# A Mamba-2, MLP and mixture-of-experts layer on one core: the first MLP four steps later, and other banks for early sums and transposes

## The chip, the cores and the metric

One core of one Trainium2 chip runs the whole program in one launch. The number that counts is device time in microseconds, as the median of several runs; lower is better. The engines named below are PE (TensorE: matrix products and transposes), DVE (VectorE), ACT (ScalarE), POOL (GpSimd) and SP (SyncE, which here only issues DMAs). Each works through its own list of instructions in order, and waits on semaphores for the others. [...]

## The reference, cut to what matters

The input x has 2048 tokens of 512 numbers. All arithmetic is fp32.

```
h   = layernorm(x); h1 = rmsnorm(h, ln1_w)
z, xb, B, C, dt = split(h1 @ in_proj_w)        # 512 -> 1024 + 256 + 256 + 1024 + 16
xb, B, C = silu(causal_conv4(xb, B, C))
dt  = softplus(dt + dt_bias);  dA = dt * -exp(A_log)
# 16 chunks of 128 tokens, 16 heads of 64, state 64 x 64 per head:
Y   = C B^T * exp(cum differences of dA) * dt @ xb  +  C @ state * exp(cum dA)
state = exp(sum dA) * state + B^T (decay * dt * xb)
y   = rmsnorm((Y + D * xb) * silu(z), norm_w) @ out_proj_w      # 1024 -> 512, "po" below
h   = h + y
x   = x + h + mlp(rmsnorm(h, ln2_w))            # silu(. @ gate) * (. @ up) @ down, 2048 wide
out = x + experts(layernorm(x))                 # 8 experts of width 352, the best 2 per token
```

## The kernel before

**Blocks and chunks.** The Mamba part runs over 8 blocks of 256 tokens (`TB`), each of two chunks of 128 (`t` = 0 to 15). For a block, `prepare(b)` computes the norm's scales, transposes the two chunks of normed tokens (`transposed`, tile `pt`, into `hT`), the step sizes dt (`pdt`, L228, and a chain of some twenty small DVE operations, L238 to L259, ending in `dA`), and their running sums (`pc`, L262, `pn`, `psum`). `spread(b, j)` brings these sums back from HBM broadcast to all partitions: two DMAs `cum` and four `ec`, with a POOL select behind each `cum`. `project` makes the channels xb, B, C (tiles `pm`, six pairs, weights `wi` loaded by SP in three buffers, each pair with a convolution of eight DVE operations and a SiLU on ACT); `gate` makes z (tiles `pz`, four pairs, with SiLU).

**A chunk's pieces.** `chunk` is a generator of nine pieces: the score products `psc` (L400), the exponentials (L406, ACT) and their products (L408, DVE); the state's part of Y (`py`, L423), then the chunk's own part (`py`, L431) and the new state `pst`; both for two halves of the heads; then the squares for the norm, `po` (L475, eight products of 512 columns), the norm's scale `ry` from `pms` (L478, a square root on ACT), h (L484, which reads `po`), h's own scale r (again a square root), and as the ninth piece the transposes of h into `h2T`, which feed the MLP.

**The MLP.** `feed_forward(fb)` works on 512 tokens (two blocks), also as a generator: 16 column groups of four pieces and one closing piece, 65 in all. It uses seven products where a plain computation would use eight (sums of blocks, made by `sums` and on POOL for the weights). Two banks, `px` and `py_c` (kinds "g" and "u" in `use`, pool `ps_x`), take these products; `pd` (kind "d", pool `ps_mm`) takes the down projection. Nothing uses "g" and "u" before the first MLP starts.

**The order.** `mamba(b)` has 32 steps. In each, some of a chunk's pieces, some projections of the next block and some of `prepare(b + 1)` are issued, and after it the main loop calls `advance()`, which issues one piece of the MLP that is in turn. The first MLP begins in block 2 (`BPF` = 2), when its 512 tokens are done:

```
        for n, _ in enumerate(mamba(b)):

            if b > BPF or b == BPF and n > 1:
                advance()
```

Until block 2 a scheduler orders PE's instructions by its own costs and priorities; from block 2 on (`manual_schedule`, L887) PE's order is the order in which the program issues them. DVE, ACT and POOL are ordered by the scheduler all the way, and the small table loads of ACT (for exponential, SiLU and square root) come wherever its order changes from one function to another. MLP pieces that are left over when block 7 is done run behind it, before the last MLP and the routed experts.

**Banks.** Pool `ps_tr` has one buffer, tag "tr": the transposes of normed tokens, of h and of xb, `pdt`, `pc`, `pn`, `psum`, `pst` and `pms` follow each other in it. `ps_mm` has two, for `pm`, `pz` and `pd`. `ps_y` has one, for `py` and `po`, and at the very start for 20 transposes of the identity that depend on nothing else (L178). `ps_sg` has the scores (two banks wide), `ps_x` one for each of "g" and "u".

Line numbers in this document are those of the kernel before.

Of the kernel before, what the change touches and what calls it, by code (L numbers as in the profile page):

```python
# [8 lines left out]
F32 = mybir.dt.float32  # L9
# [6 lines left out]
P = 128  # L16
T = 2048
D = 512
NK = D // P
# [4 lines left out]
TB = 256  # L24
NCH = TB // P
NB = T // TB
FB = 512
NFB = T // FB
DFF = 2048
FH = FB // 2  # L30
FC = 128
NFC = DFF // FC
NE = 8
# [11 lines left out]
C_CW, C_CB, C_NW, C_D, C_L1, C_L2, C_DTB, C_AL = 0, 48, 60, 68, 76, 80, 84, 100  # L45
# [4 lines left out]
def mamba_mlp_moe(ctx, tc, x, w_in, w_out, w_gu, w_down, par, wr, wg, wu, wd, out):  # L50
# [3 lines left out]
    nc = tc.nc  # L54

    def bc(ap, axis, n):
        ap = ap.unsqueeze(axis)
        shape = list(ap.shape)
        shape[axis] = n
        return ap.to_broadcast(shape)  # L60
# [15 lines left out]
    def load_x(t):  # L76
        res[t] = xp.tile([P, D], F32, name=f"x{t}", tag="x")
        nc.sync.dma_start(out=res[t], in_=x[t * P : (t + 1) * P, :])

    params = pw.tile([P, NPAR], F32, name="params")  # L80
# [20 lines left out]
    ident = const.tile([P, P], F32, name="ident")  # L101
# [66 lines left out]
    ps_y = psa_stack.enter_context(tc.tile_pool(name="ps_y", bufs=1, space=PSUM))  # L168
# [3 lines left out]
    def bank(kind, shape, name):  # L172
        pool, tag = use[kind]
        return pool.tile([P, *shape], F32, name=name, tag=tag)

    idle = ps_y.tile([P, P], F32, name="idle", tag="y")
    for _ in range(20):
        nc.tensor.transpose(idle, ident, ident)  # L178

# [4 lines left out]
        nc.scalar.activation(rboth[:, lo:hi], mv[:, lo:hi, 1], AF.Sqrt, bias=eps2, scale=1.0 + EPS)  # L186
        nc.vector.reciprocal(rboth[:, lo:hi], rboth[:, lo:hi])

    def transposed(src, dst, weight=None):

        pt = bank("tr", [NK, P], "pt")
        for k in range(NK):
            nc.tensor.transpose(pt[:, k, :], src[:, k * P : (k + 1) * P], ident)  # L193
        if weight is None:
            nc.scalar.copy(dst, pt)  # L195
        else:
            nc.vector.tensor_tensor(dst, pt, bc(weight, 2, P), ALU.mult)
# [3 lines left out]
    def prepare(b):  # L201

        nonlocal first_rows
        hT = wa.tile([P, NK, TB], F32, name=f"hT{b}", tag="hT")
        hns = []
        with tc.issue_after(first_rows) if b == 1 else ExitStack():
            scales(b)
            for j in range(NCH):
                t = b * NCH + j
# [5 lines left out]
            first_rows = normed.ins  # L215
        for j in range(NCH):
            yield
            transposed(hns[j], hT[:, :, j * P : (j + 1) * P], params[:, C_L1 : C_L1 + NK])

        yield hT  # L220
        lo, hi = b * NCH, (b + 1) * NCH
# [38 lines left out]
        n = NCH * NH  # L260
# [30 lines left out]
    def spread(b, j, rows_d):  # L291

        t = b * NCH + j
        heads = rows_d[:, j * NH : (j + 1) * NH, :]
        cum = []
        for gp in range(2):
            c = wa.tile([P, 8, P], F32, name=f"cum{t}_{gp}", tag="cum", bufs=3)
            nc.sync.dma_start(out=c, in_=bc(heads[0, 8 * gp : 8 * gp + 8], 0, P))

            nc.gpsimd.affine_select(  # L300
                out=c, in_=c, pattern=[[0, 8], [1, P]], compare_op=ALU.is_ge, fill=-3.0e38,
                base=0, channel_multiplier=-1,
            )
            cum.append(c)
        ec = None
        if t:
            ec = wa.tile([P, 2, 4, P], F32, name=f"ec{t}", tag="ec")
            for g in range(4):
                part = slice(g % 2 * HD, (g % 2 + 1) * HD)
                nc.sync.dma_start(out=ec[part, g // 2], in_=bc(heads[1, 4 * g : 4 * g + 4], 0, HD))  # L310
        return cum, ec

    def finish(steps):
        while True:
            try:
                next(steps)
            except StopIteration as end:
                return end.value
# [36 lines left out]
    def gate(b, pair, hT, zs):  # L355

        pm = ps_mm.tile([P, 2, TB], F32, name=f"pz{b}_{pair}", tag="mm")
        finish(projected(b, 6 + pair, pm, hT))
        nc.scalar.activation(zs[:, 2 * pair : 2 * pair + 2, :], pm, AF.Silu)

    def channels(b):
        xb = wa.tile([P, 4, TB], F32, name=f"xb{b}", tag="xb")
        return xb, [None, None]
# [4 lines left out]
    def turned_x(t, xb):  # L368

        tok = slice(t % NCH * P, (t % NCH + 1) * P)  # L370
        pt = ps_tr.tile([P, 4, P], F32, name=f"ptx{t}", tag="tr")
        for m in range(4):
            nc.tensor.transpose(pt[:, m, :], xb[:, m, tok], ident)
        xbt = wa.tile([P, 2, 4, HD], F32, name=f"xbt{t}", tag="xbt")
        nc.scalar.copy(xbt.rearrange("p a g d -> p (a g d)"), pt.rearrange("p a q -> p (a q)"))
        return xbt
# [4 lines left out]
    def chunk(b, j, dt, ncum, dtdec, cd, cum, ec, xb, cs, zs):  # L381

        nonlocal summed
        t = b * NCH + j
# [4 lines left out]
        y = zs[:, :, tok]  # L389
# [80 lines left out]
                summed = nc.gpsimd.tensor_tensor(sq[:, 0:n, :], sq[:, 0:n, :], sq[:, n : 2 * n, :], ALU.add).ins  # L470
        yield

        po = ps_y.tile([P, D], F32, name=f"po{t}", tag="y")
        for m in range(8):
            nc.tensor.matmul(po, y[:, m, :], w_o[:, m, :], start=(m == 0), stop=(m == 7))  # L475
        yield
# [18 lines left out]
        if off == 0:  # L495
            h2T[fb] = (wk if fb % 2 else wa).tile([P, 2, NK, FH], F32, name=f"h2T{fb}", tag="h2T", bufs=1)
        half, off = divmod(off, FH)
        transposed(h, h2T[fb][:, half, :, off : off + P], params[:, C_L2 : C_L2 + NK])


# [168 lines left out]
    def sums(fb):  # L669
# [3 lines left out]
        b11, b21, b12, b22 = h[:, 0, :KH], h[:, 0, KH:], h[:, 1, :KH], h[:, 1, KH:]  # L673
        ts = wk.tile([P, 3, KH, FH], F32, name=f"ts{fb}", tag="ts", bufs=1)
        nc.vector.tensor_tensor(ts[:, 0], b12, b11, ALU.subtract)
# [12 lines left out]
    def feed_forward(fb):  # L688
# [20 lines left out]
        for c in range(NFC):  # L709
# [8 lines left out]
            if c > 1 and c % 2 == 0:  # L718
                pair = [made.pop(n) for n in (c - 2, c - 1)]
            a = wk.tile([P, 2, FH], F32, name=f"a{fb}_{c}", tag="a", bufs=4)  # L720
            up = wk.tile([P, FH], F32, name=f"up{fb}_{c}", tag="up", bufs=2)
            x1 = bank("g", [FH], f"px{fb}_{c}")
            x2 = bank("u", [FH], f"py{fb}_{c}")
# [58 lines left out]


    coming = prepare(0)
    for _ in range(3):
        hT = next(coming)
    next(coming)
    xc = channels(0)
    ready = None
    for pair in range(6):  # L790
        finish(project(0, pair, hT, *xc))
        if pair < 2:
            next(coming)
        elif pair == 2:
            ready = finish(coming)
            near = [spread(0, j, ready[-1]) for j in range(NCH)]
            nc.sync.dma_start(out=w_o, in_=w_out.rearrange("(t p) n -> p t n", p=P))
    xbts[0] = turned_x(0, xc[0])

    unweighted = list(range(8))  # L800
# [9 lines left out]
    def mamba(b):  # L810

        nonlocal ready, xc, ninth
        hT, dt, ncum, dtdec, cd, _ = ready
        xb, cs = xc
        zs = wa.tile([P, 8, TB], F32, name=f"zs{b}", tag="zs", bufs=1)
        if b + 2 < NB:
            load_x((b + 2) * NCH)
        more = b + 1 < NB
        if more:
            coming = prepare(b + 1)  # L820
            xc = channels(b + 1)
        n = 0
        for j in range(NCH):
            pieces = chunk(b, j, dt, ncum, dtdec, cd, *near[j], xb, cs, zs)
            for _ in range(4):

                if n < 2:
                    halves = (gate(b, pair, hT, zs) for pair in (2 * n, 2 * n + 1))
                elif more:
                    halves = project(b + 1, n - 2, next_hT, *xc)  # L830
                else:
                    halves = iter(())
                next(pieces)
                if more and n == 0:
                    next(coming)
                if more and n == 3:
                    next(coming)
                if b == 0:
                    weigh(1)
                yield  # L840
                next(pieces)
                if n % 4 == 0:
                    finish(ninth)
                next(halves, None)
                yield
                if more and n < 3:
                    next(coming)
                elif more and n == 3:
                    ready = finish(coming)
                next(halves, None)  # L850
                if b == 0:
                    weigh(2)
                yield
                if more and n == 0:
                    next_hT = next(coming)
                yield
                n += 1
            ninth = pieces
            if j == 0 and b + 2 < NB:
                load_x((b + 2) * NCH + 1)  # L860
            if more:
                near[j] = spread(b + 1, j, ready[-1])

    BPF = FB // TB
    ninth = iter(())
    flow = []
    tail = iter(())
# [13 lines left out]
    for b in range(NB):  # L881
        fb, at = divmod(b, BPF)
        if fb and at == 0:
            flow.append([feed_forward(fb - 1), 4 * NFC + 1])
        if b == BPF:

            in_order.enter_context(tc.manual_schedule(engines={mybir.EngineType.PE}))  # L887
        for n, _ in enumerate(mamba(b)):

            if b > BPF or b == BPF and n > 1:  # L890
                advance()
    for n in range(flow[0][1]):
        if n == 2:
# [284 lines left out]
```

## Time and profile before

| | |
|---|---|
| median of 5 runs | 1581.91 us (1580.07 to 1583.02) |
| the profiled execution | 1580.18 us, span 1578.1 us |
| mean granted clock of PE in it | 0.991 |
| PE busy | 1535.3 us, 97% |
| DVE, ACT, POOL busy | 776.8, 753.2, 403.1 us |
| bytes moved by DMA | 218.68 MB, mean 139 GB/s |
| PE idle in 0 to 60 us | 12.4 us |
| PE idle in 200 to 220 us, and granted clock there | 6.64 us, 0.74 |

The span is the time from the first to the last instruction that the profiler saw; the device time is 2.1 us longer. All times within the profile count from the span's start. Matmul records are counted twice in it (each fp32 product appears as two). A granted clock of 1.00 is full speed, and 0.50 half. "Idle before" an instruction is put down to the event that came last, so the name of a releaser is a hint, not a proof. Blocks 0 and 1 take the first 200 us, the blocks with an MLP beside them run to about 1050, the last MLP to about 1240, and the rest is experts.

### The profile page before, as it was taken

Reading aid. Unit: us, or ns where it says so; the run is one execution under the profiler, and the core shown is the slowest. Engines: PE = TensorE matmul, PEld = TensorE weight load, DVE = VectorE, ACT = ScalarE, POOL = GpSimd, SP = SyncE. Lnnn points to the kernel's source line nnn. Section 1 sums busy time; section 2 is a strip of 40 time slices with the busy share of each in tenths; the row PEclk is TensorE's granted clock in tenths of the full one; section 3 lists DMA queues with packets and bytes.
Section 4 is the critical chain, followed back from the end, with each engine's and each line's share of the span. In section 5 each row is a group of like instructions: output and inputs, shape, how many; then the busy total and the mean of one; then the engine's idle time right before and its main releaser. Section 6 shows DMA issues by size and latency. Waiting matters only on the chain. (4 is left out here: it accounts for less than half of the span.)

```text
span 1578.1 us, 19196 instructions
## 1 busy us (share of the span) xinstructions
PE 1535.3 (97%) x6303; PEld 1051.6 (67%) x6303; DVE 776.8 (49%) x2018; ACT 753.2 (48%) x1346; POOL 403.1 (26%) x510
## 2 busy tenths in 40 slices
PE   7899979999999999999999999999999999999997
PEld 6666666777666777767676777666777666555553
DVE  6876755754556364646555554434453352222221
ACT  3988896735663678457748543222211221111110
POOL 3542324423341212111212112011111123333331
PEclk8999989999999999999999999999999999999999
DMA  8443435544554443434344533238776233333332
GB/s 290 154 140 119 137 116 184 184 158 150 183 182 145 163 170 117 131 118 138 119 166 149 167 99 102 84 103 297 241 242 226 86 61 61 66 62 67 67 67 33
DMA packets 127456, 218.68 MB, mean 139 GB/s; under 512 B 11584, under 2 KB 71488, under 8 KB 127360
## 3 DMA queue, kind: packets, MB, share of 16 engines
q1 hardware_dynamic: 105088, 166.08, 32.5%
q0 software_dynamic: 8736, 20.45, 6.9%
q10 hardware_dynamic: 13536, 30.94, 5.2%
q8 instruction: 52, 0.85, 0.2%
q14 instruction: 44, 0.36, 0.1%
HBM read 176.01 MB, written 41.42 MB: 138 GB/s over the span
## 5 line engine op out<-in xcount | busy, mean ns | idle before, releaser
L685 PE MATMUL pd<-md,a 128*128 128x512 f32 x512 | 238.4, 592 | 0.0
L326 PE MATMUL pm<-hT,wi 128*128 128x256 f32 x768 | 187.2, 389 | 1.5 <-DMA wi<-in_w_in 1.5
L326 PEld LDWEIGHTS pm<-hT,wi 128*128 128x128 f32 x768 | 143.4, 194 | 26.6 <-issue 6.9
L686 DVE TENSOR_TENSOR r<-r,pd 128x512 f32<-128x512 f32 x128 | 87.6, 684 | 139.4 <-PE pd L685 138.7
L685 PEld LDWEIGHTS pd<-md,a 128*128 128x128 f32 x512 | 97.0, 190 | 74.1 <-issue 66.2
L347 DVE SCALAR_TENSOR_TENSOR ca<-pre,params,ca 128x256 f32<-128x256 f32 x288 | 134.2, 525 | 0.2
L701 PE MATMUL py<-h2T,ms 128*128 128x256 f32 x512 | 131.6, 379 | 1.6 <-POOL ms L527 0.8
L326 PE MATMUL pz<-hT,wi 128*128 128x256 f32 x512 | 118.5, 384 | 0.0
L1034 PE MATMUL epg<-ew,xgT 128*128 x312 | 118.1, 460 | 0.4 <-ACT xgT L195 0.2
L1034 PE MATMUL epu<-ew,xgT 128*128 x312 | 117.8, 459 | 0.0
L766 POOL TENSOR_TENSOR a<-a,up 128x256 f32<-128x256 f32 x64 | 46.8, 731 | 277.1 <-DVE up L760 239.0
L475 PE MATMUL po<-w_o,zs 128*128 128x512 f32 x256 | 112.8, 593 | 0.0
L406 ACT ACT_TABLE_LOAD x76 | 97.5, 1283 | 28.7 <-DVE ncum L274 19.2
L1055 PE MATMUL epd<-ew,ehT 128*128 (+1 forms) x234 | 107.1, 593 | 1.0 <-DVE ehT L1048 1.0
L701 PEld LDWEIGHTS py<-h2T,ms 128*128 128x128 f32 x512 | 95.6, 190 | 16.9 <-POOL ms L527 1.2
L326 PEld LDWEIGHTS pz<-hT,wi 128*128 128x128 f32 x512 | 95.9, 192 | 15.4 <-issue 1.9
L406 ACT ACTIVATE cum<-cum,ncum 128x128 f32<-128x128 f32 x256 | 86.3, 393 | 5.6 <-POOL cum L300 3.3
L475 PEld LDWEIGHTS po<-w_o,zs 128*128 128x128 f32 x256 | 48.2, 190 | 56.9 <-issue 55.4
L1015 POOL DMA_INDIRECT xg<-xnd,idx x39 | 38.8, 995 | 176.0 <-PE pt L193 174.0
L1034 PEld LDWEIGHTS epu<-ew,xgT 128*128 128x128 f32 x312 | 59.3, 190 | 33.0
L195 ACT COPY xgT<-pt 128x512 f32<-128x512 f32 x39 | 22.8, 587 | 117.7 <-PE pt L193 117.7
L1061 POOL DMA_INDIRECT out<-ey,idx x39 | 61.9, 1587 | 66.8 <-DVE ey L1060 40.8
(248 smaller groups left out, 2568.3 us busy)
## 6 DMA issues: line engine op xcount, KB each, us to landing
wi<-in_w_in SPq DMA_DIRECT2D x80, 512.0 KB, 3.6
ms<-late SPq DMA_DIRECT2D x48, 512.0 KB, 3.6
mg<-early SPq DMA_DIRECT2D x48, 384.0 KB, 3.6
md<-in_w_down SPq DMA_DIRECT2D x64, 256.0 KB, 3.8
cum<-rowsd SPq DMA_DIRECT2D x32, 512.0 KB, 4.1
late<-ms ACTq DMA_DIRECT2D x16, 512.0 KB, 2.7
ec<-rowsd SPq DMA_DIRECT2D x60, 128.0 KB, 3.8
xnd<-xn ACTq DMA_DIRECT2D x28, 256.0 KB, 3.5
```

The costliest lines, as they stand in the source:

```text
L326: nc.tensor.matmul(pm[:, m, :], w[:, k, m * P : (m + 1) * P], hT[:, k, :], start=(k == 0), stop=(k == NK - 1))
L347: nc.vector.scalar_tensor_tensor(ca, pre[:, m, k : k + TB], cw[:, k : k + 1], ca, ALU.mult, ALU.add)
L406: nc.scalar.activation(lt[:, half, i], lt[:, half, i], AF.Exp, bias=ncum[:, j, h : h + 1])
L475: nc.tensor.matmul(po, y[:, m, :], w_o[:, m, :], start=(m == 0), stop=(m == 7))
L685: nc.tensor.matmul(pd, a[:, j * P : (j + 1) * P], d, start=(m == 0), stop=(m == 1))
L686: nc.vector.tensor_tensor(rows[j], rows[j], pd, ALU.add)
L701: nc.tensor.matmul(ps, w[:, k], m[:, k], start=(first and k == 0), stop=(k == KH - 1), skip_group_check=True)
L766: nc.gpsimd.tensor_tensor(a[:, 1], a[:, 1], up, ALU.mult)
L1015: nc.gpsimd.indirect_dma_start(out=xg, out_offset=None, in_=src, in_offset=bass.IndirectOffsetOnAxis(ap=idx[:, n : n + 1], axis=0))
L1034: nc.tensor.matmul(ps, xT[:, k, :], w[:, lo : lo + EI], start=(k == 0), stop=(k == NK - 1))
L1055: nc.tensor.matmul(pd, hT[:n, m, :], w[:n, NG + m * D : NG + (m + 1) * D], start=(m == 0), stop=(m == len(ET) - 1))
L1061: nc.gpsimd.indirect_dma_start(out=out, out_offset=bass.IndirectOffsetOnAxis(ap=idx[:, n : n + 1], axis=0), in_=y, in_offset=None, compute ...
```

## The change

Four edits, one patch.

1. The second of block 0's two sets of transposes goes to a bank of `ps_mm` (kind "d") instead of the "tr" bank, and five more transposes of the identity, into `ps_y`, follow it.
2. The `spread` of block 0's second chunk is issued behind the six projection pairs of block 0 instead of behind the third.
3. `po` of the first four chunks (blocks 0 and 1) goes to the bank "g" instead of `ps_y`.
4. The first MLP piece is issued behind the seventh step of block 2 (`n > 5`) instead of the third (`n > 1`); the ninth piece of chunk 3, which in other blocks is issued in the second quarter of a block's first step group, is issued in block 2 at the end of it, three steps later. All later MLP pieces move with the first, so nine instead of five are left over behind block 7.

```diff
+BPF = FB // TB
...
-    idle = ps_y.tile([P, P], F32, name="idle", tag="y")
-    for _ in range(20):
-        nc.tensor.transpose(idle, ident, ident)
+    def idling(n):
+        idle = ps_y.tile([P, P], F32, name="idle", tag="y")
+        for _ in range(n):
+            nc.tensor.transpose(idle, ident, ident)
+
+    idling(20)
...
-    def transposed(src, dst, weight=None):
-
-        pt = bank("tr", [NK, P], "pt")
+    def transposed(src, dst, weight=None, kind="tr"):
+
+        pt = bank(kind, [NK, P], "pt")
...
-            transposed(hns[j], hT[:, :, j * P : (j + 1) * P], params[:, C_L1 : C_L1 + NK])
+            kind = "d" if b == 0 and j else "tr"
+            transposed(hns[j], hT[:, :, j * P : (j + 1) * P], params[:, C_L1 : C_L1 + NK], kind)
+            if b == 0 and j:
+                idling(5)
...
-        po = ps_y.tile([P, D], F32, name=f"po{t}", tag="y")
+
+        po = ps_y.tile([P, D], F32, name=f"po{t}", tag="y") if t >= BPF * NCH else bank("g", [D], f"po{t}")
...
-            near = [spread(0, j, ready[-1]) for j in range(NCH)]
+            near = [spread(0, 0, ready[-1])]
             nc.sync.dma_start(out=w_o, in_=w_out.rearrange("(t p) n -> p t n", p=P))
+    near.append(spread(0, 1, ready[-1]))
...
-                if n % 4 == 0:
+                if n % 4 == 0 and (b != BPF or n):
                     finish(ninth)
...
                 yield
+                if b == BPF and n == 0:
+                    finish(ninth)
                 n += 1
...
-            if b > BPF or b == BPF and n > 1:
+            if b > BPF or b == BPF and n > 5:
                 advance()
```

More of the change, by code (lines that the diff above doesn't have):

```diff
@@ L862, in mamba @@
                 near[j] = spread(b + 1, j, ready[-1])
-    BPF = FB // TB
     ninth = iter(())
```

## The prediction

> **What bounds the kernel now.** I read the page first: the busy line, then the slices (one is 39.5 us).
>
> ```profile
> PE 1535.3 (97%) x6303; PEld 1051.6 (67%) x6303; DVE 776.8 (49%) x2018; ACT 753.2 (48%) x1346; POOL 403.1 (26%) x510
> ...
> PE   7899979999999999999999999999999999999997
> ...
> ACT  3988896735663678457748543222211221111110
> ...
> PEclk8999989999999999999999999999999999999999
> ```
>
> PE is the bound: 97% busy, and nearly all of what it misses lies in slices 1 and 2 (the start), 6 (197 to 237 us) and 40 (the end, which the change leaves alone). An edit that only reorders PE work is therefore worth the PE idle time that it removes, plus the half-clock time that follows such idle time. ACT, 48% busy over all, is near 90% in slices 2 to 6, so it can take PE's place there.
>
> Next, who PE waited for (total, times, longest):
>
> ```profile
> PE pt L193 <- DVE mv L145: 7.1, 1, 7.1
> PE py L423 <- POOL halo L340: 3.8, 2, 2.4
> PE pc L262 <- POOL pre L339: 3.4, 1, 3.4
> PE pt L193 <- DVE hT L197: 1.9, 1, 1.9
> PE pt L193 <- ACT xbt L375: 1.7, 1, 1.7
> ```
>
> The five sum to 17.9 us; the timeline places them at 199.6, 121.1 and 197.0, 24.8, 7.3 and 41.2. Third, the timeline around the largest (start, length, what; in brackets the idle time before it):
>
> ```profile
> 197.58 0.75 DVE L484 SCALAR_TENSOR_TENSOR h<-po,ry,h 128x512 f32<-128x512 f32 x1
> ...
> 198.43 1.13 PE L423 MATMUL py<-ec,sdiag 128*128 128x128 f32 x8 [1.39 <-POOL halo L340]
> ...
> 204.04 0.29 ACT L139 ACTIVATE r<-m,singles 128x1 f32<-128x1 f32 x1
> ...
> 206.04 0.46 DVE L492 TENSOR_SCALAR h<-h,r 128x512 f32<-128x512 f32 x1
> ...
> 206.64 1.09 PE L193 MATMUL pt<-ident,h 128*128 128x128 f32 x4 [7.08 <-DVE mv L145]
> ...
> 207.52 5.00 PE L326 MATMUL pz<-hT,wi 128*128 128x256 f32 x16
> ...
> 220.38 1.08 PE L431 MATMUL py<-cum,xbt 128*64 128x512 f32 x4
> ```
>
> The 7.08 us is chunk 3's last step: its h is ready at 206.50 (206.04 + 0.46), and PE's written order has nothing in front of it but work already done. The name DVE mv is only the last event seen. The 1.39 us is a bank: L423 starts 0.10 after the read of po at L484 ends (198.33), for po and py share the one buffer of ps_y. The same pair stands at 123.49 (L484 ends at 123.39), where the wait is 2.43. Fourth, stretches of PE alone (length, busy, matmuls, granted clock, DMA share, GB/s):
>
> ```profile
> 1.50:2.50 1.00, 0.97 (x5) 1.00 0.58 199
> ...
> 8.00:9.10 1.10, 0.00 (x0) 0.92 0.87 175
> ...
> 11.00:12.70 1.70, 1.66 (x8) 0.50 1.07 406
> ...
> 199.00:202.00 3.00, 0.56 (x6) 0.68 0.23 89
> 202.00:206.00 4.00, 0.00 (x0) 0.50 0.38 133
> ```
>
> Idle time costs twice: the clock falls to half in the gap at 7.3 and recovers near 19; it falls in the gap at 199.6 and is full again by 212.
>
> **Part 1: first transposes in two banks, five idle transposes.** Before, the second set of four waits for the hT product at L197 (8.41 to 9.09) to free the one "tr" bank, so it runs at 9.14 and its own product at 10.29, behind two hn products (L211, 1.00 for both) that DVE's order put between. After, the second set follows the first at 7.3 in an "mm" bank, which nothing uses yet. DVE's new order has both products in a row: 8.41, 9.00, done at 9.69. So pdt (L228) starts at 9.75, not 11.04: 1.29 earlier. The five idle transposes (4.33/20 = 0.22 each, 1.1) lie in the 1.9 us between and cost nothing; without that gap they cost 1.1.
>
> What follows depends on the clock. At half, pdt takes its 3.60 again and the 3.44 wait of pc at 28.24 just ends 1.29 sooner. At full, pdt takes 1.85 (as at 64.96). The 8 matmuls of pm_0, done at about 20.4 (its copy starts at 20.52), take 3.62 (as at 71.79) and end near 15.2; the DVE chain from there to dA (21.21 to 28.1, 6.9) ends near 22.9, so pc comes 5.2 earlier. DVE's order also puts the statistics of chunk 4 (2.29 waiting for a DMA at 17.1) behind dA; that wait lay before 21.21, so it is no extra. Behind pc the new order has pm_5 between two halves of ptx and the next hn transposes later. That removes 1.73 (ptx's bank) and, as wi leaves SP's queue ahead of the moved spread, 1.48 (wi). It adds about 1.2 before py, whose eight exponentials ACT spreads between SiLUs: 2.0 net, 1.7 taken. The term lies between 3.0 (half clock) and 6.9 (full). The gap of 0.77 at 5.85 left the clock at 1.00 and the 1.87 gap did not; after, the gap is 0.75, but pdt is thin work. I take 4.5; for the range, 0 (DVE at 17.5 and ACT at 19.3 of 20 us busy in 40 to 60 allow nothing) to 7.
>
> [...]
>
> **Part 2: second chunk's spread later.** Two cum DMAs (512 KB), four ec DMAs (128 KB) on SP, and two selects on POOL (1.09 each) move behind the projections of block 0. SP now issues wi for pairs 5 and 6 ahead of cum1_0 (before: 39.93, behind an ec issue of 37.46); counted in part 1. Chunk 1 first needs cum1_0 at about 71 (its first exponential); issue near 33 and 4.1 to land leave over 30 us of cover. Cost 0; if cover were gone, 4.1 + 1.09.
>
> **Part 3: po of chunks 0 to 3 in bank "g".** No instruction more. L423 no longer waits for L484: 2.43 at 123.49 goes (1.39 at 198.43 is counted below). What could be late next: ec is done at 117.1, sdiag at 108.1, and chunk 2's h transposes need ry, which stood on ACT behind three exponentials and a table load (119.78, 0.98, and 1.28) that the new order puts after it. So I take all 2.4; bounds 0 and 2.43. A new wait, po's for the read of the po before, has 25 us of cover or more (po at 111.25, the read before it at 86.3). The first MLP product in that bank comes about 24 us after the last read.
>
> **Part 4: first MLP four steps later, chunk 3's last step after three more.** PE's new order in block 2, walked with the old durations from the shared point (psc ends at 197.0): py 1.05 to 198.1 without the bank wait; pz_0 3.62 to 201.7; hn transposes 0.60; pz_1 3.62 to 205.9. DVE is busy with cum (to 204.3) and xd (205.4), then r's reciprocal, hT 0.69 (206.3), h 0.46 (206.7). The second hn set runs at 206.4, its hT on DVE behind 0.54 and 0.67 at 208.0 to 208.7; h's transposes end at 209.4; py 1.08, pst 1.03, psc 1.13 to 212.6; the next py waits for yd (1.12 behind 0.69 + 0.69) and ends at 213.8; pz_2 3.62, pdt 1.85, pz_3 3.62: 222.8. Before, pz_3 ends at 235.76 with seven products of the MLP's first piece in front of it, 0.865 apart, 6.1: equal to 229.7. Gain 6.9. It is the two waits (8.5) and the half clock (pz_0 5.00 against 3.62, pt 1.09 against 0.60: 1.9), less 3.5 of new waits on DVE and ACT. The moved pieces come back behind block 7: four more, 9.8 (1048.22 to 1057.99), with as much less in the blocks between; PE is full there, so the net is 0. ACT's queue is what stands behind: from 206.2 to the SiLU of pz_3 it has 8 table loads (1.28) and 5.3 of work, 221.7, one us ahead of PE. Bounds: 0 to 8.8.
>
> SP's and POOL's orders around FB boundaries shift by one piece; the waits there are nine of 0.5 to 0.85, so ±1.5; I take 0.
>
> **Sum.** 4.5 + 2.4 + 6.9 = 13.8. The profiled execution took 1580.18 (span 1578.1, 2.1 around it), 1.7 below the median of 1581.91. So 1566.4 beside that one, 1568.2 in median.
>
> **Rivals.** *Front gives nothing* (DVE and ACT bound 40 to 60): 1581.9 - 9.3 = 1572.6. For: those busy shares. Against: ACT is idle for 9.5 of the 20 us before that (10.54 busy in 20 to 40). *The clock stays full*: front 7 and block 2 near 8: 1564. *Block 2 gains only half*, a new wait at py or pdt taking the rest: 1572. *Slower*: ACT bounds block 2. It is busy 19.56 of 20 us in 200 to 220; if pz_3 still ends at 235.8, the 6.1 taken out of PE there leaves a hole, and comes back after block 7. The start's gains then drain into the same wait on ACT: 1581.9 + 6.1 = 1588. It decides once pz_3 ends 6.9 (the other two terms) later than 229.7. Against: ACT's sum above. *It doesn't act*: po's bank moves the wait only; the cover of part 3 excludes that.
>
> **How the numbers follow.** About 0.2% (3.2 us) is the least that can be told from no change. Forecast 0.50 (1565 to 1571), front nothing 0.15, clock full 0.13, half of block 2 0.12, slower 0.07, other losses that cancel the gain 0.03. Faster 0.90, same 0.03, slower 0.07. The range takes the sums with the ends: 1560 (7 + 2.4 + 8.8 + 1.5 off gives 1562.2, and the runs of one kernel spread by some 2 below their median) to 1577 (5 of 13.8 left).
>
> **What would show it.** Right: in the waits of PE the 7.1 of pt and both py L423 rows are gone; pdt starts before 10; MLP products begin after pz_3, near 215 on the new axis; clock 1.00 from 200 to 220. Wrong: a PE wait of over 3 us on ACT or DVE in 200 to 240, or pc not earlier than 27. I am wrong most easily where DVE's and ACT's written orders turn a short delay into a long one.

## The result, and the profile after

The changed kernel took 1587.16 us in the median of 22 runs (1582.48 to 1591.81), the kernel before 1582.17 us beside it (43 runs, 1579.17 to 1585.17): a ratio of 1.0032, with a 95% interval of 1.0025 to 1.0038. It is 5.0 us slower; the forecast was 13.8 us faster, with a range that ended at 1577.

The profiled execution took 1585.92 us (span 1583.9), 5.7 above that of before. Its page, busy line and three slices (line numbers of the changed kernel are up to 10 higher than those of before):

```profile
PE 1538.8 (97%) x6308; PEld 1049.9 (66%) x6308; DVE 780.7 (49%) x2018; ACT 749.4 (47%) x1343; POOL 403.2 (25%) x510
...
PE   8999989999999999999999999999999999999996
...
ACT  5988987645744775557367542222211221111110
...
PEclk9999999999999999999999999999999999999999
```

At this grain the start and block 2 look better (slices 1, 2 and 6 of PE), only the last slice reads one lower, and PE is as busy as it was. The loss shows only in PE's waits (what was waited for: total, times, longest):

```profile
PE pt L197 <- ACT cd L295: 5.2, 3, 2.4
PE py L709 <- DVE a L742: 3.5, 1, 3.5
PE pc L269 <- DVE dA L266: 3.2, 3, 1.9
PE px L709 <- ACT a L754: 3.1, 5, 1.9
PE pt L197 <- DVE hT L201: 2.6, 2, 2.3
```

The rows that the prediction wanted gone are gone: the 7.1 us of h's transposes, both waits of the state product for the y bank, the 3.4 us of `pc`. But the first two rows here are new, and they stand where the prediction did not look, behind block 2. The timeline of PE from the last score products in front of block 2 (start, length, what; in brackets the idle time before it; an fp32 product of PE makes two records, the eight of `po` in 16 chunks 256 on the page, and numbers of its products below are numbers of records):

```profile
189.74 1.13 PE L407 MATMUL psc<-cs,xb 64*128 64x512 f32 x4
...
202.40 0.80 PE L197 MATMUL pt<-ident,h 128*128 128x128 f32 x4 [2.33 <-DVE hT L201]
...
213.71 3.70 PE L333 MATMUL pz<-hT,wi 128*128 128x256 f32 x16
...
228.38 0.41 PE L269 MATMUL pc<-tri,dA 128*32 128x128 f32 x2 [1.55 <-ACT xbt L382]
...
234.36 1.13 PE L709 MATMUL px<-ts,mg 128*128 128x256 f32 x4 [1.93 <-ACT a L754]
```

The same score products in the kernel before:

```profile
195.91 1.13 PE L400 MATMUL psc<-cs,xb 64*128 64x512 f32 x4
```

Here ends block 1's part: PE has by then done the same work in both kernels, but for the five idle transposes. The changed kernel is 6.2 us ahead (190.87 against 197.04). Its last gate products end at 217.41, against 229.7 in the kernel before for the same work (the prediction's figure): 12.3 us ahead, of the 13.8 forecast. Then two waits of ACT, 3.5 together, come within 20 us. How the lead goes on is read from the start of each chunk's `pms`, changed kernel less before, with 9.8 us added from chunk 5 on, since four MLP pieces fewer lie in front of it (the four last ones, 1048.22 to 1057.99 in the trace of before). Chunk 3's `pms` is 8.4 us earlier, but that is not for equal work: ten more records of projections, 2.2 us, are still to come behind it.

| chunk | block 1's end | 5 | 8 | 10 | 11 | 12 | 13 | 14 | 15 |
|---|---|---|---|---|---|---|---|---|---|
| us, for equal work | -6.2 | -9.0 | -6.7 | -8.1 | -5.4 | -2.5 | -1.6 | +4.0 | +5.7 |

So 6.2 us were won up to block 1's end, block 2 added 2.8 net (6.1 up to the gate products, of which 3.3 went again behind them), and 14.7 were lost between chunks 5 and 15. Behind chunk 15 nothing changes any more. Between 240 and 1080 us PE is idle for 12.2 us after and 4.7 before; the stretches below (length, PE busy, matmuls, granted clock, DMA share, GB/s), PE alone, of the changed kernel, show the rest, a clock below full:

```profile
480.00:560.00 80.00, 77.05 (x338) 1.00 0.46 153
...
700.00:860.00 160.00, 156.47 (x657) 0.99 0.40 134
860.00:1000.00 140.00, 136.46 (x572) 0.98 0.36 115
```

In the kernel before, the same three stretches have 79.34, 160.00 and 139.24 us busy and a clock of 1.00. One hundredth of 160 us and two of 140 are some 4 us, so 7.5 + 4 of the 14.7 are seen directly; the rest is spread thinly, or within what one profiled execution differs from another. The largest single wait, by engine (PE's row after DVE's and POOL's, all of the same 10 us):

```profile
968.56 2.36 DVE L665 TENSOR_TENSOR v<-o,oh 128x256 f32<-128x256 f32 x2
970.84 2.08 DVE L666 TENSOR_TENSOR v<-v,wt 128x256 f32<-128x256 f32 x2
972.85 1.81 DVE L668 TENSOR_TENSOR v<-v,place 128x256 f32<-128x256 f32 x2
974.59 0.67 DVE L694 TENSOR_TENSOR r<-r,pd 128x512 f32<-128x512 f32 x1
975.18 0.41 DVE L742 TENSOR_TENSOR a<-a,py 128x256 f32<-128x256 f32 x1
...
968.43 2.81 POOL L477 TENSOR_TENSOR sq<-sq 128x512 f32<-128x512 f32 x3 [6.41 <-ACT sq L475]
971.19 2.85 POOL L402 TENSOR_TENSOR ec<-ec,cs 128x512 f32<-128x512 f32 x2
...
975.65 2.07 PE L709 MATMUL py<-h2T,ms 128*128 128x256 f32 x4 [3.54 <-DVE a L742]
977.51 1.91 PE L709 MATMUL px<-ts,ms 128*128 128x256 f32 x4
```

PE waits for a small MLP addition on DVE (L742), and that stands in DVE's list behind six products `v` of the routing step. The six take 6.25 us here; elsewhere they take 2.3 (median 0.42 each). Meanwhile POOL is at work on a chunk's squares and on `ec`. Behind the wait the granted clock is 0.50 (974.5 to 981.0): four products (two groups of them) that need 1.03 take 2.07 and 1.91.

The second kind of new wait, three times, around 545 us (ACT's rows, then PE's):

```profile
542.18 1.28 ACT L140 ACT_TABLE_LOAD   x1
543.48 0.29 ACT L140 ACTIVATE r<-m,singles 128x1 f32<-128x1 f32 x1
543.79 1.28 ACT L289 ACT_TABLE_LOAD   x1
545.09 0.20 ACT L289 ACTIVATE dtdec<-psum 128x32 f32<-128x32 f32 x1
545.18 0.35 ACT L295 ACTIVATE cd<-psum 64x16 f32<-64x16 f32 x2
...
539.95 0.30 PE L287 MATMUL psum<-dA,late 128*128 128x32 f32 x2
...
545.59 0.66 PE L197 MATMUL pt<-ident,xn 128*128 128x128 f32 x4 [2.44 <-ACT cd L295]
```

`psum` and the routing step's transposes use the same one bank "tr", which comes free when ACT has read `psum` (545.53). The kernel before has the same ACT rows, 16.5 us later (`psum` at 556.49, `cd` done at 562.08); but its PE had a down projection of four products and `pl` in between and came to those transposes only at 563.10, one us after the bank was free. Nothing became slower. The MLP, with the routing steps that ride on it, came four pieces later against the Mamba steps, and now meets them elsewhere.

### The profile page after: what moved, and what is told of

Same layout as the page of the kernel before. It is cut to its first block, busy times and chain, and to the rows that moved or that the text cites. A ratio compares the mean times of both kernels' runs of the same rounds, so it can differ in the third digit from the quotient of the medians.

```text
span 1583.9 us, 19202 instructions
## 1 busy us (share of the span) xinstructions
PE 1538.8 (97%) x6308; PEld 1049.9 (66%) x6308; DVE 780.7 (49%) x2018; ACT 749.4 (47%) x1343; POOL 403.2 (25%) x510
## 5 line engine op out<-in xcount | busy, mean ns | idle before, releaser
L354 DVE SCALAR_TENSOR_TENSOR ca<-pre,params,ca 128x256 f32<-128x256 f32 x288 | 138.2, 538 | 0.3
L333 PEld LDWEIGHTS pz<-hT,wi 128*128 128x128 f32 x512 | 94.8, 190 | 13.8 <-ACT zs L366 0.8
L754 ACT COPY a<-px 128x256 f32<-128x256 f32 x64 | 23.6, 369 | 142.9 <-PE px L709 124.7
```

The lines of the kernel that those rows point to most:

```text
L333: nc.tensor.matmul(pm[:, m, :], w[:, k, m * P : (m + 1) * P], hT[:, k, :], start=(k == 0), stop=(k == NK - 1))
L354: nc.vector.scalar_tensor_tensor(ca, pre[:, m, k : k + TB], cw[:, k : k + 1], ca, ALU.mult, ALU.add)
```

## The experiments

Three theories. *Lag*: parts 1 to 3 give what they give, and the loss behind block 2 comes from the MLP and the routing steps standing four pieces later against the Mamba steps. *Lists*: the new orders on DVE, ACT and POOL, which the scheduler makes from the whole program, cost the time, whatever the lag. *One queue*: a single resource, the bank "tr" or DVE beside POOL, makes the loss. The kernel before took 1582.6 us beside the first four runs, 1582.92 beside the next four, 1582.37 beside the last four.

**Parts 1 to 3 alone.** The changed kernel without part 4: the MLP begins where it did before.

```diff
-            if b > BPF or b == BPF and n > 5:
+            if b > BPF or b == BPF and n > 1:
...
-                if n % 4 == 0 and (b != BPF or n):
+                if n % 4 == 0:
...
-                if b == BPF and n == 0:
-                    finish(ninth)
```

> Parts 1 to 3 (two banks and five idle transposes, the later spread, po in bank g); the first MLP starts where it did before. Theory 'lag': the early gains are real and the loss comes from the MLP running one column group later. Then chunk 3's norm product pms is again about 8.4 us earlier than before, the 7 us wait for chunk 3's h stays, no wait above 1 us stands behind 540 us, and the time is 1582.2 - 8.4 = 1573.8 (1571 to 1577). Rival 'lists': the new orders of DVE, ACT and POOL that come with parts 1 to 3 make the late waits; then waits above 2 us stand behind 540 us and the time is 1582 to 1587.

Measured: 1573.65 us (1571.78 to 1575.26), ratio 0.994 (0.9927 to 0.9952). Its lead is 2.7 us at block 1's end in this execution (chunk 3's `pms` is 5.4 us earlier, not 8.4), and from chunk 5 to chunk 15 its `pms` are 5.4 to 4.6 us ahead, flat. Behind 540 us no wait reaches 0.8 us up to 1080. The wait for h stays, shorter:

```profile
200.23 1.08 PE L197 MATMUL pt<-ident,h 128*128 128x128 f32 x4 [4.81 <-DVE h L500]
```

So block 2 gave 2.7 us here without part 4, and 2.8 in the changed kernel with it.

**Part 4 alone.** The reverse of it: the kernel before with the MLP and chunk 3's last step later.

```diff
-            if b > BPF or b == BPF and n > 1:
+            if b > BPF or b == BPF and n > 5:
...
-                if n % 4 == 0:
+                if n % 4 == 0 and (b != BPF or n):
...
+                if b == BPF and n == 0:
+                    finish(ninth)
```

> The kernel before with part 4 alone: first MLP behind the seventh step of block 2, chunk 3's last step later. Lag: the early gains of parts 1 to 3 (8.4) are missing and the late loss is there: 1587.2 + 8.4 = 1595.6 (1588 to 1598), with waits above 2 us behind 540 us. Lists: the wait for h goes and nothing is given back: 1582.2 - 4 to 7 = 1575 to 1578.

Measured: 1594.24 us (1589.74 to 1596.86), ratio 1.0066 (1.0052 to 1.0081). Part 4 costs 11.6 us by itself and 13.5 on top of parts 1 to 3. Its new waits are those of the changed kernel (what, total, times, longest):

```profile
PE pt L194 <- ACT cd L289: 4.4, 2, 2.5
...
PE py L702 <- DVE a L735: 3.5, 1, 3.5
```

**The lag made up within block 2.** Four steps of block 2 issue two MLP pieces, so from block 3 on everything stands as before.

```diff
             if b > BPF or b == BPF and n > 5:
                 advance()
+            if b == BPF and n in (13, 18, 23, 28):
+                advance()
```

> The changed kernel, with four of block 2's later steps (13, 18, 23, 28) issuing two MLP pieces instead of one, so that from block 3 on MLP and Mamba stand to each other as before. Lag: the gain of 12.3 us that stood at pz_3 of block 2 is kept, less the two waits of 226 to 234 us (3.5): 1570 to 1574, and the waits of 2.4 (545.6), 2.3 (850.7) and 3.5 us (975.6) are gone. Lists: about 1587, with those waits.

Measured: 1578.05 us (1575.32 to 1580.9), ratio 0.9967 (0.9954 to 0.9979). From chunk 5 on its `pms` are flat, 0.5 to 0.9 us behind those of before; the waits of 2.4 and 3.5 us are gone. So the loss behind block 2 is the lag's. But block 2 keeps nothing either: in this execution PE was level with before (0.2 us behind) at block 1's end and is 0.5 behind at chunk 5. The time is 4.4 us above that of parts 1 to 3 alone.

**The lag made up in block 3.**

```diff
             if b > BPF or b == BPF and n > 5:
                 advance()
+            if b == BPF + 1 and n in (5, 13, 21, 29):
+                advance()
```

> The changed kernel, whose MLP makes up its four pieces in the next block (block 3, one extra piece at each of four steps eight apart) and not within block 2; from block 4 on the MLP and the routing steps stand against the Mamba steps as before. Theory (the loss behind block 2 comes from the lag alone; what the front and block 2 gave is kept once the lag is gone): in the changed kernel chunk 5's states' products came 18.8 us earlier than before with about 9.8 us less MLP in front of them, so 9.0 us are there to keep, and no late waits: 1573 (1570 to 1577), and the waits of over 2 us at 545, 850 and 975 us gone. Rival (the pieces made up cost their time again wherever they are put, as they seemed to in block 2): 1577 to 1583. Rival (the loss sits in the new order of the lists, whatever the lag): 1585 to 1588.

Measured: 1577.91 us (1574.06 to 1578.22), ratio 0.9961 (0.9949 to 0.9974). Its lead for equal work is 9.2 us at chunk 5, as in the changed kernel, and flat at 6.1 from chunk 8 to 15. The lists theory falls (it gave 1585 to 1588). The rival that the pieces cost their time wherever they are put is right in part: 3.1 us of the lead go in blocks 3 and 4, in and behind the stretch where the pieces are made up. Within block 2 the same waits stand as in the changed kernel:

```profile
204.11 0.66 PE L197 MATMUL pt<-ident,h 128*128 128x128 f32 x4 [2.34 <-DVE hT L201]
...
228.45 0.41 PE L269 MATMUL pc<-tri,dA 128*32 128x128 f32 x2 [1.55 <-ACT xbt L382]
...
234.45 1.13 PE L709 MATMUL px<-ts,mg 128*128 128x256 f32 x4 [1.94 <-ACT a L754]
```

They sum to 5.8, against 4.8 of one wait for h in the kernel with parts 1 to 3 alone. Taking that one wait away by moving the MLP bought three others.

**Half the lag.** The changed kernel with the MLP two pieces later than before, not four.

```diff
-            if b > BPF or b == BPF and n > 5:
+            if b > BPF or b == BPF and n > 3:
```

> The changed kernel with the MLP two pieces later than before in place of four (it begins at step 4 of block 2, chunk 3's last step still at the end of the first column group). Theory that any lag puts the routing steps' ACT and DVE work beside Mamba's dense steps, and that the size of the loss goes by where they land: half a column group is another place, so waits of 1.5 to 3.5 us in some of the four routing stretches, in other places than with four pieces; 1578 to 1588, I take 1582. Rival (loss in proportion to the lag): parts 1 to 3 alone measured 1573.7, the whole change 1587.2, so half way, 1580. Rival (only a lag of a whole group meets the transposes' bank behind the states' sums): 1570 to 1575, since the waits at 545 and 850 us would go and block 2 keep some of its gain.

Measured: 1597.4 us (1592.61 to 1601.41), ratio 1.0088 (1.007 to 1.0107). Worse than four pieces, and outside all three expectations: the loss is not in proportion to the lag, and it is not special to a whole group of four. With 4.9 us for its two missing pieces, its lead of 5.1 at block 1's end is 2.9 at chunk 5, a delay of 3.9 at chunk 8 and of 14.4 at chunk 15. Its largest wait, rows of DVE and then of PE:

```profile
412.67 0.69 DVE L145 BATCH_NORM_STATS2 bn<-x 128x6 f32<-128x512 f32 x1 [2.11 <-DMA x<-in_x]
...
415.75 1.27 DVE L354 SCALAR_TENSOR_TENSOR ca<-pre,params,ca 128x256 f32<-128x256 f32 x3
416.94 0.41 DVE L773 TENSOR_TENSOR a<-a,px 128x256 f32<-128x256 f32 x1
...
417.40 2.07 PE L709 MATMUL px<-h2T,mg 128*128 128x256 f32 x4 [4.11 <-DVE a L773]
```

Here the addition for which PE waits stands in DVE's list behind the statistics of a new chunk, which wait for a load, and a run of convolution products. It is another queue again, with the same shape: an urgent small operation of the MLP behind Mamba work that it used to precede.

**The routing step one piece away.** The changed kernel; the routing steps ride on another of each four pieces, so that their transposes no longer come right behind `psum`.

```diff
-        if now[1] % 4 == 1:
+        if now[1] % 4 == 0:
             next(tail, None)
```

> The changed kernel, with the routing step that runs beside each MLP column group issued behind the group's first piece instead of behind its last but one count (one step later). Lag, by way of the tr bank: the route's transposes no longer stand right behind psum, so the 2.44 at 545.6, the 0.72 at 697.9, the 2.31 at 850.7 and the half clock behind the last (1.7) go: 1587.2 - 7.2 = 1580. If the bank is not the cause, these waits stay and the time is 1587.

Measured: 1586.68 us (1579.72 to 1589.47), ratio 1.0016 (1.0005 to 1.0026): as the rival had it. The three waits for ACT's `cd` vanish (2.44, 0.72 and 2.31). Others come, some at the same bank "tr" (1.60 us at 829 for `pc`, which was 0.95, and 0.80, 0.67 and 0.67 at 844, 867 and 902), the largest at 858 us, with four products behind it that take 2.07 us instead of 1.03:

```profile
858.52 2.07 PE L709 MATMUL px<-h2T,mg 128*128 128x256 f32 x4 [3.26 <-DVE a L773]
```

So the three waits that were seen do not carry the loss by themselves: with the routing steps in another place, other waits take it up. In the changed kernel, in this one and with half the lag, the largest waits behind 240 us stand at two kinds of places, the bank "tr" and DVE's `a`, so the one-queue theory does not hold for either alone. What a kernel would gain with DVE's products alone out of POOL's way was not tried.

**POOL beside the routing products.** The kernel before; in the first of the two passes POOL squares the one-hot tile in place twice, while DVE makes the products `v`. Ones and zeros stay what they are.

```diff
+            if n == 0:
+                for _ in range(2):
+                    nc.gpsimd.tensor_tensor(ohl, ohl, ohl, ALU.mult)
             vs = []
```

> The kernel before, where in each of the two routing passes' first one POOL squares the one-hot tile in place (128x512, twice; its ones and zeros stay what they are) while DVE makes the six v products; the second pass is left as it is. Theory that DVE's products slow beside POOL's: the first pass's products under POOL take 1.0 to 1.5 us each, those of the second pass 0.42 us as in the kernel before. Rival (the slow products at 968 us in the changed kernel had another cause, such as their inputs or a DMA): 0.42 us in both passes.

Measured, first pass (DVE, then POOL):

```profile
659.85 1.59 DVE L660 TENSOR_TENSOR v<-o,oh 128x256 f32<-128x256 f32 x2
661.37 1.59 DVE L661 TENSOR_TENSOR v<-v,wt 128x256 f32<-128x256 f32 x2
662.88 0.75 DVE L663 TENSOR_TENSOR v<-v,place 128x256 f32<-128x256 f32 x2
...
660.01 2.33 POOL L654 TENSOR_TENSOR ohl<-ohl 128x512 f32<-128x512 f32 x2 [9.69 <-DVE ohl L651]
```

Two products that take 0.75 when POOL is still take 1.59 while it runs, twice over, and the third pair, after POOL has ended, 0.75 again; the second pass has 0.76 for all three pairs. In the first pass at 962 us POOL's squares came only behind the products, and all three pairs took 0.75. So POOL's work beside them slows these products (one of each pair to 1.26, the other not). Beside the slow products at 968 us POOL was at work too, on other tiles. (One execution, 1585.73 us.)

**Part 1 alone.**

```diff
-            transposed(hns[j], hT[:, :, j * P : (j + 1) * P], params[:, C_L1 : C_L1 + NK])
+            kind = "d" if b == 0 and j else "tr"
+            transposed(hns[j], hT[:, :, j * P : (j + 1) * P], params[:, C_L1 : C_L1 + NK], kind)
+            if b == 0 and j:
+                idling(5)
```

> The kernel before with part 1 alone: the first block's second transposes in the other pool's bank and five idle transposes behind them. The prediction gave this 4.5 us: 1578.1 by the median of 1582.6. The trace of the changed kernel has pdt 2.1 us and pc 7.4 us earlier, and the four parts 1 to 3 together measured 8.9; with part 3 at its predicted 2.4, part 1 would be 6.5: 1576 (1574 to 1578.5). Rival: the wait for the wi transfer behind chunk 0 takes most of it back (it stood at 1.5 us in the kernel before and 2.6 to 4.9 where parts 1 to 3 were in): 1579 to 1581.

Measured: 1572.15 us (1571.57 to 1573.77), ratio 0.9931 (0.9918 to 0.9944). It gains 10.8 us, more than any expectation and no less than parts 1 to 3 together. The wait for the `wi` transfer is not among its waits; but behind `pc` the second normed tokens' transposes wait 1.61 us at 33.8 and 4.61 at 39.0, and the lead of 7.4 us at `pc` is 6.5 at block 1's end.

```profile
8.92 2.01 PE L234 MATMUL pdt<-w_dt,hT 128*128 128x16 f32 x16 [0.48 <-DVE hT L200]
...
20.82 0.38 PE L268 MATMUL pc<-tri,dA 128*32 128x128 f32 x2 [0.39 <-DVE dA L265]
...
197.89 1.08 PE L196 MATMUL pt<-ident,h 128*128 128x128 f32 x4 [3.21 <-DVE h L498]
```

`pc` comes 7.4 us earlier than before (28.24). At block 2 the wait for h is 3.21, not 7.08, but the wait for the y bank just in front of it is 3.01 (at 193.55), not 1.39: together 6.2 against 8.5. ACT's new order has three table loads between `pms` and h's scale where there were four, and h is ready 7.2 us behind the end of the score products (190.54 to 197.74), where it was after 9.5 (197.04 to 206.50). The lead is 8.1 from chunk 5 to the end. The median says 10.8, the one profile 8.1.

**Part 1 without the idle transposes.**

```diff
             transposed(hns[j], hT[:, :, j * P : (j + 1) * P], params[:, C_L1 : C_L1 + NK], kind)
-            if b == 0 and j:
-                idling(5)
```

> Part 1's second bank without its five idle transposes. The prediction put most of part 1's gain on the bank and on pdt at the full clock (its 16 products took 1.96 us behind the idle transposes, 3.6 in the kernel before at half the clock). Theory (the idle transposes keep the clock up until pdt): without them pdt takes 3.3 to 3.7 us again, 1573.5 to 1575. Rival (the clock is up without them): pdt at 2.0 us and 1571.5 to 1572.7.

Measured: 1573.26 us (1570.76 to 1574.47), ratio 0.9937 (0.9924 to 0.995). It lies between the two expectations: the 1.1 us that the idle transposes seem to give is within the intervals, and 9.1 us come with the bank alone. `pdt` takes 2.72 (2.01 with them), and `pc` comes at 22.64, 1.8 later than with them.

**Part 3 alone.**

```diff
-        po = ps_y.tile([P, D], F32, name=f"po{t}", tag="y")
+        po = ps_y.tile([P, D], F32, name=f"po{t}", tag="y") if t >= 4 else bank("g", [D], f"po{t}")
```

> The kernel before with part 3 alone: the first four chunks' projections summed in the MLP's idle bank. Prediction: 2.4 us less, 1580.4 by the median of 1582.8. Rival, since parts 1 to 3 together (1573.7) measured no less than part 1 alone (1572.2): what part 3 saves at the y bank is lost at the next wait of these chunks (h's norm, the wi transfer): 1582 to 1584.

Measured: 1585.31 us (1584.18 to 1587.14), ratio 1.0013 (1.0005 to 1.0022): 2.9 us slower by the medians, 0.8 to 3.5 by the interval, a little past the rival. The y bank's waits are gone; PE comes earlier to h's transposes, and waits there (PE, then ACT):

```profile
129.47 0.63 PE L193 MATMUL pt<-ident,h 128*128 128x128 f32 x4 [2.12 <-DVE h L492]
...
210.55 1.09 PE L193 MATMUL pt<-ident,h 128*128 128x128 f32 x4 [8.21 <-DVE mv L145]
...
200.94 0.26 ACT L139 ACTIVATE ry<-pms,singles 128x1 f32<-128x1 f32 x1
```

Gone are 2.43 and 1.39 us. New are 2.12 here and 0.88 at 172.2, and the 8.21 was 7.08: 3.8 out, 4.1 in. ACT has an exponential and a table load more between `pms` and `ry` than it had (4.7 us from 196.25 here, 2.3 from 194.73 before). The rest of the loss these waits don't show: in this execution PE is 2.5 us behind the kernel before already at its first score products (51.05 against 48.57), ahead of any `po`, and so it is (50.93) in the trace of part 4 alone, whose start has the code of before.

**Parts 1 and 3, without part 2.** The parts 1 to 3 with both spreads together again.

```diff
-            near = [spread(0, 0, ready[-1])]
+            near = [spread(0, j, ready[-1]) for j in range(NCH)]
...
-    near.append(spread(0, 1, ready[-1]))
```

> Parts 1 and 3 without part 2 (both chunks' spreads stand together again). Parts 1 to 3 measured 1573.7, part 1 alone 1572.2. If part 2 costs the 1.5 us between them: 1570 to 1572.3. If part 3 costs it: 1573.7 (1572.8 to 1575).

Measured: 1574.33 us (1572.1 to 1576.38), ratio 0.9948 (0.9936 to 0.9961). Part 3 adds no gain to part 1: 8.0 with it, 10.8 without. Whether it costs something is not settled, for the two intervals just overlap and the two profiled executions are equal (1572.20 and 1572.15). The waits again only move: the 3.01 at the y bank is gone, and h's transposes wait 6.66, where part 1 alone had 3.01 + 3.21:

```profile
198.69 1.09 PE L197 MATMUL pt<-ident,h 128*128 128x128 f32 x4 [6.66 <-ACT cs L360]
```

Part 2 makes no difference that these runs tell (8.9 with it, 8.0 without, intervals overlapping).

**Part 1, and chunk 3's last step later without the MLP.** h's four transposes go behind the first sixteen gate products and the second hn transposes, still ahead of the MLP, which begins where it did.

```diff
-                if n % 4 == 0:
+                if n % 4 == 0 and (b != BPF or n):
                     finish(ninth)
...
                 elif more and n == 3:
                     ready = finish(coming)
+                if b == BPF and n == 0:
+                    finish(ninth)
                 next(halves, None)
```

> Part 1 alone, and of part 4 only that chunk 3's last step (its four transposes of h) stands later in block 2's first column group: behind the second hn transposes, between the first and the second sixteen gate products, and so still ahead of the MLP, which begins where it did before. Part 1 alone waits 3.2 us for h at 197.9 us with sixteen gate products of 5.1 us ready behind it. Theory (the wait itself was real time, only the MLP's lag lost it again): 1572.2 less 3 = 1569 (1567.5 to 1570.5), and no new waits of over 1.5 us behind 210 us. Rival (the time comes back at the next thing that is late, such as the second transposes' copy or the half clock up to 210 us, whatever the MLP does): 1571 to 1573.

Measured: 1569.35 us (1567.82 to 1570.46), ratio 0.9913 (0.99 to 0.9926), 13.0 us faster than before and the best of all these kernels.

```profile
194.56 1.33 PE L430 MATMUL py<-ec,sdiag 128*128 128x128 f32 x8 [3.01 <-issue]
195.68 5.14 PE L333 MATMUL pz<-hT,wi 128*128 128x256 f32 x16
200.66 0.60 PE L197 MATMUL pt<-ident,hn 128*128 128x128 f32 x4
202.04 0.66 PE L197 MATMUL pt<-ident,h 128*128 128x128 f32 x4 [0.79 <-DVE hT L201]
```

The wait of 3.21 has become 0.79, the median is 2.8 lower (2.2 when each is taken against the kernel before beside it), and PE's idle time from 240 to 1080 us stays at 5.2 (5.4 with part 1 alone). Block 2 gives 4.4 us here, from 5.5 ahead at its start to 9.9 at chunk 5. So the time at h was real, and the MLP didn't have to move for it. The 3.01 is the y bank's wait: DVE's read of `po` ends at 194.45. Part 3 takes that wait away, and with h's transposes later it might now gain; this was not run.

## Why the prediction was wrong

| part | predicted | measured |
|---|---|---|
| 1, two banks and idle transposes | -4.5 (0 to -7) | -10.8 alone |
| 2, spread later | 0 | not told from 0 |
| 3, po in bank "g" | -2.4 (0 to -2.4) | +2.9 alone (0.8 to 3.5), not told from 0 on part 1 |
| 4, MLP and last step later | -6.9 (0 to -8.8) | +11.6 alone, +13.5 on parts 1 to 3 |
| sum | -13.8 | +5.0 |

**The step that failed** is in part 4: "The moved pieces come back behind block 7 ... PE is full there, so the net is 0", and with it "SP's and POOL's orders around FB boundaries shift by one piece; the waits there are nine of 0.5 to 0.85, so ±1.5; I take 0". The first counts PE's work and is right about that: the 9.8 us came back where I said. But a full PE means that the other lists happen to deliver in time at the old alignment; it says nothing of another one. The second looked only at SP and POOL and at the size of the old waits. What was shifted was the whole MLP with the routing steps, on DVE and ACT as well, for 840 us. The runs showed in its place a loss of 11.6 us with the lag alone and 13.5 on top of parts 1 to 3; with the lag made up, the loss behind block 2 is gone (twice); with half of it, it is larger. The prediction's own sign of being wrong, "a PE wait of over 3 us on ACT or DVE in 200 to 240", looked at the wrong stretch: the one wait over 3 us stands at 975.

**Part 4 within block 2.** The walk up to the last gate products was good: 26.5 us from the end of the score products, 25.8 in the walk; 12.3 us ahead at 217.4, 13.8 forecast; and MLP products from 217.25 ("near 215"). It stopped there, as if that point set the end. Right behind it the lead met ACT, as the walk's last sentence on ACT, "one us ahead of PE", could have said: 1.55 and 1.93 of waits, and block 2 as a whole gave 2.8, no more than without part 4 (2.7). The granted clock from 200 to 220 is 0.91, not 1.00. The move of the last step alone, without the MLP, gives 2.2 to 2.8 on part 1.

**Part 1** had the mechanism right and its size too low. `pdt` starts at 8.90 ("9.75"; "before 10" as a sign) and takes 2.0 (1.85 at full clock), `pc` is 7.4 us earlier (5.2 in the better of the two cases). I took a middle value between full and half clock, where full came true for `pdt`; and a part of the gain, 1.6 us, appears only at block 2, with ACT's new order around `ry` and h, which I had not walked for this part. What was to go behind `pc`, "1.73 (ptx's bank)" and "1.48 (wi)", did not: part 1 alone waits 1.61 and 4.61 there. So the 10.8 did not come by the terms that were written down: what comes up to `pc` was too low, and what was to come behind it had the wrong sign.

**Part 3** failed at "I take all 2.4". The wait did go, as said. What is late next was asked for the exponentials and chunk 2's `ry`, with an order of ACT that belonged to all parts together; h's transposes of chunks 1 and 3 were not asked for, and their waits take it all back (3.8 out, 4.1 in). The rival "po's bank moves the wait only" was given no price; the traces of part 3 alone and on part 1 both show it.

**The rivals.** "Front gives nothing" is refuted by part 1 alone. "Slower, 1588" is near the measured time, but not by its mechanism: its point of decision was gate products ending 6.9 us later than 229.7, and they ended at 217.4. Up to there ACT did not bound block 2; the gain drained afterwards, over many stretches, into DVE, ACT and the bank "tr". Only "other losses that cancel the gain", with 0.03 and no mechanism, comes near it; the chance of 0.07 for slower stood on a cause that did not act.

## What to carry to other kernels

When two streams of work are interleaved by hand, shifting one against the other is a change to every stretch where both run, whatever it saves where it begins. Price it by that: walk one period of the new alignment on each in-order engine and look for small urgent operations that now stand behind long runs of the other stream, and for single buffers that now pass from one stream to the other. If the wait to be filled needs only a few instructions moved, move those and leave the phase alone, as the last experiment does. And a wait removed at a bank may be worth nothing, as here, until the next instruction that joins the same chain, here h's transposes behind ACT's work for h, is earlier too.

## What the runs showed of the hardware

**DVE's products took longer beside POOL's.** In the kernel before, each of DVE's 48 products `v` of 128x256 took 0.42 to 0.43 us. With POOL's two squares of 128x512 put beside them (2.33 us for both), one of each of the first two pairs took 1.26, and the pair 1.59 instead of 0.75. In the changed kernel at 968 us, beside a chunk's squares (2.81) and `ec` (2.85), the six took 1.49, 0.94, 0.68, 1.48, 1.48 and 0.41. The longest is longer by 1.1. What in POOL's work holds them up, no run shows.

**At the start the clock was at half for 10.2, 6.8 or 3.4 us.** In the first 20 us of the kernel before, the mean granted clock is 0.93 from 8.5 to 9.0 us, 0.50 from 9.0 to 19.0 and 0.83 from 19.0 to 19.5; worked out from this, it is at half for 10.2 us (8.9 to 19.2). In the same way it is at half for 6.8 us (10.1 to 16.9) with two banks and no idle transposes, and for 3.4 with part 1 alone (10.7 to 14.1) and in the changed kernel (11.6 to 15.0): three, two and one times 3.4. The mean of 0 to 20 us is 0.74 in the kernel before and with part 3 alone, 0.83 with the bank alone, and 0.91 in the changed kernel, with part 1 alone, with parts 1 and 3, and with part 1 and the last step later. The length of a wait did not decide by itself: one of 2.44 us at 545 left the granted clock at 1.00 (1.03 for four products), one of 2.31 at 850 in the same trace left 0.50 for 3.4 us (851.3 to 854.7), and one of 3.54 at 975 stood in a stretch at 0.50 of 6.8 us (974.2 to 981.0). With the five idle transposes the time was about 1.1 us lower, within the intervals; whether they keep the clock up, these runs do not settle.

**The start varies from one execution to the next.** Five profiled kernels have the same order on every engine up to chunk 3: the changed one, the two that make up the lag, the one with half of it and the one with the routing step moved. At block 1's end they are 6.2, -0.2, 4.5, 5.1 and 0.8 us ahead of the one profile of before. So leads of a few us in a single profile are no measure of a gain; single profiles were used here for where time goes, and medians for how much.
